# Six token tiles in one Sinkhorn chain on VectorE, instead of a second chain on GpSimd

## The chip, the cores and the metric

The kernel runs on one core of a Trainium2 chip. The metric is the device time of one execution in microseconds, the median of the runs. Besides the times there is one profiled execution, taken by the hardware profiler; all durations below come from it. Engines are named as in the profile: PE is TensorE, DVE is VectorE, ACT is ScalarE, POOL is GpSimd, SP is the engine that issues the DMAs.

## The reference, cut to what matters

Two adaLN layers follow each other on an input of 2 batch rows x 512 tokens x 512 features. Layer 0 is a gated linear attention with 32 heads and a feed-forward product. Layer 1 is an attention over the tokens, and then a mixing of four residual streams. That last step is where the change is made. For each token the 512 features are taken as n = 4 streams of C = 128:

```python
H_res_logits = (x_norm @ W_res.T).reshape(B, T, n, n) + H_res_base
H_pre  = softmax(x_norm @ W_pre.T  + H_pre_base)        # 4 per token
H_post = softmax(x_norm @ W_post.T + H_post_base)       # 4 per token
# Sinkhorn: 50 times rows, then columns, of a 4 x 4 matrix per token
u = -logsumexp(Z + v[..., None, :], axis=-1)
v = -logsumexp(Z + u[..., :, None], axis=-2)
H_res = (1 - g) * I + g * exp(Z + u[..., :, None] + v[..., None, :])
y = einsum('btnc,btn->btc', x_streams, H_pre) @ W_branch
out = einsum('btij,btjc->btic', H_res, x_streams) + einsum('btc,btn->btnc', y, H_post)
```

The 50 Sinkhorn steps of a token depend on each other; different tokens are independent. So the work is a long chain of very small instructions, each of which can take several token tiles at once.

## The kernel before

A token tile is 128 tokens, one on each partition. There are eight: tiles 0 to 3 of batch row 0 and tiles 0 to 3 of batch row 1. A framework schedules the traced instructions: priorities and a planned time line set a fixed order on each engine, and at run time each engine goes through its own list in that order, waiting on semaphores.

The last stage of the kernel begins when layer 1's attention has finished a half of a batch row (two tiles). For each pair of tiles there is then:

- `opening` (L966): transposes, a small product, statistics and the 24 logits of each token, the two softmaxes, and the branch `y` (tile `yb`).
- `first_iteration` (L1083): the first Sinkhorn step, with maxima and logarithms.
- `iterations` (L1106): the other 49 steps in linear form. A step is a product by the column factors (L1129), a sum of rows (L1119), a reciprocal (L1131), a product by the row factors (L1133), a sum of columns (L1119) and a reciprocal (L1135). Each needs the one before. After the steps named in `RENEW` (16 and 32) two logarithms and an exponential on ACT rebuild the matrix (L1139, L1111 to L1114).
- `result` (L1143): the mixing matrix (L1146, L1147, L1150).
- the mixing: `mixed_on_tensor` (L1171) writes 16 diagonal matrices per tile with ACT (L1161) and multiplies them on PE with the streams into one PSUM tile (L1182), and 4 more for the branch, unless the branch has been put into the PSUM tile before by `branch_on_tensor` (L1163). `mixed_on_vector` (L1197) does a tile with 16 DVE instructions (L1202) instead. `put` (L1153) multiplies by the gate on DVE (L1156), adds the residual on POOL or DVE (L1157) and stores the tile.

With `last=False` the products and sums of a chain run on POOL (L1129, L1133, L1122, L1123) and only the reciprocals run on DVE; with `last=True` everything runs on DVE.

Before the change the four pairs go like this:

- `streams0(0)` and `streams0(2)`: row 0, first and second half. Each has its own chain of two tiles on POOL (with reciprocals on DVE), and then its own two mixings on PE.
- `streams1a`: row 1, first half (called A below). It makes a room for four tiles, and runs steps 1 to 16 (`HEAD`) for its two tiles on DVE.
- `streams1b`: row 1, second half (called S below). After its `opening` and `first_iteration` it runs a joint chain of four tiles for 33 steps. Then A has had its 50 steps and is mixed, while S runs its last 16 steps with two tiles. At the end S's tile 1 is mixed on PE, its tile 0 on DVE.

`part(R, lo, hi)` takes some of the tiles of a room. `aside` (L1260) draws the next pieces of these generators into the trace, with raised priority.

Of the kernel before, what the change touches and what calls it, by code (L numbers as in the profile page):

```python
# [9 lines left out]
FP = mybir.dt.float32  # L10
# [6 lines left out]
UPS = 400, 400, 400, 400  # L17
RATES = None, None, None, None
HEAD = 16
UP = 400  # L20
# [16 lines left out]
P = 128  # L37
B, L, HID = 2, 512, 512
NC = L // P
# [4 lines left out]
NS, NITER = 4, 50  # L44
# [8 lines left out]
def tile_adaln(ctx: ExitStack, tc: tile.TileContext, a: dict, out: bass.AP):  # L53
    nc = tc.nc
# [6 lines left out]
    psp = ctx.enter_context(tc.tile_pool(name="ps", bufs=2, space=PSUM))  # L61
# [89 lines left out]
    def temp(shape, dt, name, bufs=2):  # L151
        return wk.tile(shape, dt, name=name, bufs=bufs)
# [202 lines left out]
    ps = bank([64, HID], "mps")  # L355
# [609 lines left out]

    def opening(S, last):  # L966

        b, c0, n = S["b"], S["c0"], S["n"]
        t0 = b * NC + c0
# [5 lines left out]
        for kc in range(KC):  # L975
            ps = psp.tile([P, n * P], FP, name="hps")
# [49 lines left out]
        nc.vector.tensor_tensor(sm, sm, m8.unsqueeze(3).to_broadcast(s8), ALU.mult)  # L1026
        yield

        yb = temp([P, 4, P], FP, "yb", 3)[:, 0:n]
        for c in range(n):  # L1030
            xp = temp([P, P], FP, "xp")
            if XP or b:
# [18 lines left out]
            yield  # L1051
        S.update(h=h, xs=xs, lg=lg, sm=sm, yb=yb)

# [6 lines left out]

    def chain_room(n, last):

        room = temp([P, 512], FP, "sinkhorn", 4)
        used = [0]

        def carve(shape):
            m = int(np.prod(shape[1:]))
            t = room[:, used[0]:used[0] + m]
            used[0] += m
            if len(shape) == 4:  # L1070
                return t.rearrange("p (c i j) -> p c i j", i=NS, j=shape[3])
            return t.rearrange("p (c i) -> p c i", i=NS)

        R = {k: carve([P, n, NS, NS]) for k in ("z", "t", "y", "K")}
        R.update({k: carve([P, n, NS]) for k in ("mx", "s", "u", "v", "fa", "fb", "fl")})
        if not last:
            R["pairs"] = carve([P, n, NS, 2])
        return R

    def part(R, lo, hi):  # L1080
        return {k: t[:, lo:hi] for k, t in R.items()}

    def first_iteration(S, R):  # L1083
        z, t, y, K, mx, s_, u, v, fl = (R[k] for k in ("z", "t", "y", "K", "mx", "s", "u", "v", "fl"))
        nc.vector.tensor_scalar(
            z, S["lg"][:, :, 0:16].rearrange("p c (i j) -> p c i j", j=NS), INV_TAU, None, ALU.mult
        )

        def minus_lse(dst, y, inv=None):
            nc.vector.tensor_reduce(mx, y, AX.X, ALU.max)  # L1090
            nc.vector.tensor_tensor(t, y, over(mx), ALU.subtract)
            act(t, t, AF.Exp)
            nc.vector.tensor_reduce(s_, t, AX.X, ALU.add)
            if inv is not None:
                nc.vector.reciprocal(inv, s_)
            act(s_, s_, AF.Ln)
            nc.vector.scalar_tensor_tensor(dst, mx, -1.0, s_, ALU.mult, ALU.subtract)

        minus_lse(u, z)
        yield  # L1100
        nc.vector.tensor_tensor(y, z, over(u), ALU.add)
        minus_lse(v, tp_(y), fl)
        nc.vector.tensor_tensor(K, tp_(t), along(fl), ALU.mult)
        yield

    def iterations(R, its, renew, last):  # L1106

        z, t, K, u, v, fa, fb, fl = (R[k] for k in ("z", "t", "K", "u", "v", "fa", "fb", "fl"))
        big = nc.vector if last else nc.gpsimd

        def kernel_of():  # L1111
            nc.vector.tensor_tensor(K, z, over(u), ALU.add)
            nc.vector.tensor_tensor(K, K, along(v), ALU.add)
            act(K, K, AF.Exp)  # L1114

        def sums(dst, y):

            if last:
                nc.vector.tensor_reduce(dst, y, AX.X, ALU.add)  # L1119
            else:  # L1120
                h2 = R["pairs"]
                nc.gpsimd.tensor_tensor(h2, y[:, :, :, 0:2], y[:, :, :, 2:4], ALU.add)  # L1122
                nc.gpsimd.tensor_tensor(dst, h2[:, :, :, 0], h2[:, :, :, 1], ALU.add)  # L1123

        for it in its:
            if it == 1 or it - 1 in renew:
                sums(fa, K)
            else:
                big.tensor_tensor(t, K, along(fb), ALU.mult)  # L1129
                sums(fa, t)  # L1130
            nc.vector.reciprocal(fa, fa)  # L1131
            yield
            big.tensor_tensor(t, tp_(K), along(fa), ALU.mult)  # L1133
            sums(fb, t)
            nc.vector.reciprocal(fb, fb)  # L1135
            if it in renew:
                for d, f in ((u, fa), (v, fb)):
                    act(fl, f, AF.Ln)
                    nc.vector.tensor_tensor(d, d, fl, ALU.add)  # L1139
                kernel_of()  # L1140
            yield

    def result(S, R):  # L1143

        hr, n = R["y"], S["n"]
        nc.vector.tensor_tensor(hr, R["K"], over(R["fa"]), ALU.mult)  # L1146
        nc.vector.tensor_tensor(hr, hr, along(R["fb"]), ALU.mult)  # L1147
        hrf = hr.rearrange("p c i j -> p c (i j)")
        for c in range(n):
            nc.vector.scalar_tensor_tensor(hrf[:, c, :], hrf[:, c, :], gt[:, 0:1], diag, ALU.mult, ALU.add)  # L1150
        S["hr"] = hr
# [10 lines left out]

    def branch_on_tensor(S, c):  # L1163

        S["ps", c] = mps = psp.tile([P, NS, P], FP, name="mixb", bufs=1)
        dg = wts.tile([P, NS + 1, P], FP, name="dg", bufs=2)
        for i in range(NS):
            diagonal(dg[:, i], S["sm"][:, c, 1, i:i + 1])
            nc.tensor.matmul(mps[:, i], lhsT=dg[:, i], rhs=S["yb"][:, c], start=i == 0, stop=False)
# [21 lines left out]
    def branch_on_scalar(S, c):  # L1191

        S["f", c] = f = wts.tile([P, NS, P], FP, name="foutb", bufs=1)
        for i in range(NS):
            nc.scalar.activation(f[:, i], S["yb"][:, c, :], AF.Copy, scale=S["sm"][:, c, 1, i:i + 1])
# [13 lines left out]

    RENEW = 16, 32  # L1210

    def streams0(c0):

        S = {"b": 0, "c0": c0, "n": 2}
        yield from opening(S, False)
        R = chain_room(2, False)
        yield from first_iteration(S, R)
        yield from iterations(R, range(1, NITER), RENEW, False)
        result(S, R)
        for c in range(2):  # L1220
            yield from mixed_on_tensor(S, c, nc.gpsimd)

    joint = {}

    def streams1a():

        S = joint["a"] = {"b": 1, "c0": 0, "n": 2}
        yield from opening(S, True)
        R = joint["R"] = chain_room(4, True)
        yield from first_iteration(S, part(R, 0, 2))  # L1230
        yield from iterations(part(R, 0, 2), range(1, HEAD + 1), (HEAD,), True)

    def streams1b(ahead):

        S = {"b": 1, "c0": 2, "n": 2}
        yield from opening(S, True)
        yield from ahead
        A, R = joint["a"], joint["R"]
        yield from first_iteration(S, part(R, 2, 4))
        branch_on_tensor(S, 1)  # L1240
        branch_on_scalar(S, 0)
        yield from iterations(R, range(1, NITER - HEAD), RENEW, True)
        result(A, part(R, 0, 2))
        side.append((None, mixed_on_tensor(A, 0, nc.gpsimd), UP))
        side.append((None, mixed_on_tensor(A, 1, nc.gpsimd), UP))
        yield from iterations(part(R, 2, 4), range(NITER - HEAD, NITER), RENEW, True)
        result(S, part(R, 2, 4))
        last = [mixed_on_tensor(S, 1, nc.vector), mixed_on_vector(S, 0)]
        while last:
            for e in list(last):  # L1250
                if next(e, "end") == "end":
                    last.remove(e)
            yield
# [4 lines left out]
    side = []  # L1258
# [51 lines left out]
    def weighed():  # L1310
        w = wt[0]
        wt[0] += 1
        if w < n_pieces:
            if w == n_pieces // 2:
                row_tiles(1, (GA,))
                values1(1)
            weigh(order[w // 8], w % 8)
        o = w - OUT
        if 0 <= o < n_pieces and o % 4 == 3:
            outputs(o // 4)  # L1320
        o -= 5
        if o >= 0 and o % 4 == 0 and o < n_pieces:
            j = o // 4
            finish(j)
            if j % 16 == 5:
                with behind():
                    row_tiles(j // 16, (SB, CB, GB))
                    weights24(j // 16)
            if j % 8 == 7:
                k = j // 8  # L1330
                if k == 2:
                    joint["ahead"] = streams1a()
                side.append((RATES[k], (streams0(2 * k) if k < 2 else joint["ahead"] if k == 2 else streams1b(joint["ahead"])), UPS[k]))

    virtual = []
    load_stationary("wk0", 0, 0)
# [37 lines left out]
    for n, u in enumerate(units):  # L1374
        g, b, c = u["at"]
# [128 lines left out]
```

## Time and profile before

| | |
|---|---|
| runs of the kernel before | 1398.12 us median of 3 (1397.33 to 1403.47) |
| the profiled execution | 1401.8 us; its span from first to last instruction is 1400.0 us |
| busy, share of the span | PE 89%, DVE 83%, ACT 59%, POOL 55% |
| granted TensorE clock, mean | 0.948 |

Busy time of the engines in five stretches of the end (from windows of the trace):

| stretch, us | what runs | PE | DVE | ACT | POOL |
|---|---|---|---|---|---|
| 1195 to 1258 | attention of row 1, both POOL chains | 59.40 | 55.37 | | 38.57 |
| 1258 to 1296 | end of attention, A's 16 steps, S's opening | 18.29 | 32.80 | 17.05 | 30.23 |
| 1296 to 1359 | the joint chain of four tiles | 11.44 | 54.95 | 14.98 | 44.70 |
| 1359 to 1387 | S's last 16 steps, mixings | 19.89 | 23.83 | 21.01 | 6.28 |
| 1387 to 1400 | the last tiles | 8.55 | 8.56 | 8.01 | 3.33 |

The shares over the whole span say little here: the change lies in the last 200 us, where other engines are busy than before. In a row of a timeline the first number is the start of the instruction, the second its duration, and the bracket at the end is the idle time of the engine before it with what ended it. An instruction's duration includes its latency, so two that don't depend on each other can overlap on one engine, and the step from one start to the next is what a chain pays. In a row of a group the numbers behind the bar are the busy time of the group and the mean ns of one.

### The profile page before, as it was taken

How to read it: one execution, taken by the hardware profiler on the slowest of the kernel's cores; microseconds unless marked ns; L12 is line 12 of the kernel's file. 1: busy time of each engine (PE TensorE's matmuls, PEld its weight loads, DVE VectorE, ACT ScalarE, POOL GpSimd, SP SyncE). 2: the span in 40 equal slices, each digit the busy share in tenths (PEclk: the TensorE clock that was granted, in tenths of full speed). 3: DMA queues.
4: the chain of work that ended last, by engine and by line, in shares of the span. 5: the costliest groups of instructions: out<-in, count | busy, mean ns of one | idle time of the engine just before them, and what ended most of it. 6: DMA issues, size and time to landing. Idle time of an engine off the chain costs nothing. (4 is left out here: it accounts for less than half of the span.)

```text
span 1400.0 us, 22901 instructions
## 1 busy us (share of the span) xinstructions
PE 1245.7 (89%) x7168; PEld 992.1 (71%) x7168; DVE 1159.8 (83%) x2969; ACT 831.5 (59%) x2354; POOL 775.8 (55%) x1169
## 2 busy tenths in 40 slices
PE   5979999999999999999988999799999889994128
PEld 3758888788788778888866777577676666663117
DVE  7998668687677687787899977688799979898887
ACT  5457576476376466666665656557567467664128
POOL 4454374364264367577777748545242655558861
PEclk9989999999999999999999999999999999997568
DMA  8022241231142343324333317523203231200001
GB/s 256 23 65 60 88 121 30 68 107 53 53 118 57 92 120 106 98 68 124 118 114 91 98 53 241 170 67 91 90 24 113 71 111 52 59 11 1 1 16 46
DMA packets 95377, 117.13 MB, mean 84 GB/s; under 512 B 10828, under 2 KB 50508, under 8 KB 95256
## 3 DMA queue, kind: packets, MB, share of 16 engines
q1 hardware_dynamic: 95256, 115.67, 27.7%
q8 instruction: 57, 0.93, 0.3%
q14 instruction: 64, 0.52, 0.1%
HBM read 102.11 MB, written 10.64 MB: 81 GB/s over the span
## 5 line engine op out<-in xcount | busy, mean ns | idle before, releaser
L846 DVE TENSOR_REDUCE m<-s 128x1 f32<-128x512 f32 x256 | 166.4, 673 | 18.6 <-PE s L842 18.3
L67 ACT ACTIVATE pt<-s 128x512 f32<-128x512 f32 x256 | 136.9, 602 | 33.3 <-PE s L876 31.7
L447 POOL TENSOR_TENSOR q<-xcos,rot 128x512 f32<-128x512 f32 x64 | 92.8, 1450 | 61.6 <-DVE xcos L445 57.1
L67 ACT ACTIVATE sg<-sg 128x512 f32<-128x512 f32 x128 | 80.6, 632 | 68.5 <-DVE sg L478 66.8
L876 PE MATMUL s<-qs,ks 100*128 100x256 f32 x512 | 103.3, 306 | 11.0 <-DMA qs<-mm 7.4
L842 PE MATMUL s<-ks,qs 96*128 96x512 f32 x256 | 103.6, 437 | 9.7 <-DVE m L846 7.5
L515 POOL TENSOR_TENSOR gb<-gb,q 128x512 f32<-128x512 f32 x48 | 63.2, 1319 | 77.7 <-ACT gb L67 68.7
L232 PE MATMUL pps<-hh,wq_h 128*128 128x512 f32 x256 | 103.2, 403 | 1.7 <-ACT vT L766 1.1
L876 PEld LDWEIGHTS s<-qs,ks 100*128 100x128 f32 x512 | 80.9, 195 | 33.5 <-ACT pt L67 8.9
L232 PE MATMUL gps<-wg_h,hh 128*128 128x512 f32 x256 | 101.8, 400 | 2.9 <-ACT wg_h L209 2.7
L232 PE MATMUL ops<-wo_h,zh 128*128 128x512 f32 x256 | 101.5, 397 | 1.7 <-ACT zh L570 1.0
L232 PE MATMUL ops<-wo_h,zl 128*128 128x512 f32 x256 | 100.8, 394 | 0.7 <-DVE zl L571 0.7
L232 PE MATMUL pps<-hl,wq_h 128*128 128x512 f32 x256 | 101.3, 396 | 0.0
L232 PE MATMUL pps<-hh,wq_l 128*128 128x512 f32 x256 | 101.2, 395 | 0.0
L232 PE MATMUL gps<-wg_l,hh 128*128 128x512 f32 x256 | 101.2, 395 | 0.0
L232 PE MATMUL gps<-wg_h,hl 128*128 128x512 f32 x256 | 100.6, 393 | 0.0
L232 PE MATMUL ops<-wo_l,zh 128*128 128x512 f32 x256 | 99.9, 390 | 0.0
L67 ACT ACTIVATE dec<-dec,room 128x128 f32<-128x128 f32 x256 | 83.0, 398 | 21.8 <-POOL dec L495 21.7
L548 PE MATMUL yps<-v,dec 128*128 128x128 f32 x512 | 94.2, 280 | 1.8 <-DVE xcos L445 1.0
L495 POOL TENSOR_SCALAR_AFFINE_SELECT dec<-gb 128x512 f32<-128x512 f32 x64 | 49.1, 768 | 80.7 <-DMA gb<-g_dram 51.8
L522 POOL TENSOR_TENSOR xw<-v,room 128x512 f32<-128x512 f32 x48 | 55.2, 1163 | 68.5 <-ACT v L462 64.3
L558 DVE SCALAR_TENSOR_TENSOR z<-yps,ss,sg 128x128 f32<-128x128 f32 x256 | 71.9, 340 | 24.0 <-ACT ss L67 23.8
(323 smaller groups left out, 3968.5 us busy)
## 6 DMA issues: line engine op xcount, KB each, us to landing
gb<-g_dram SPq DMA_DIRECT2D x64, 256.0 KB
raw<-in_wq SPq DMA_DIRECT2D x56, 256.0 KB
raw<-in_wg SPq DMA_DIRECT2D x48, 256.0 KB
raw<-in_wo SPq DMA_DIRECT2D x48, 256.0 KB
raw<-in_wmod SPq DMA_DIRECT2D x40, 256.0 KB
qs<-q_dram SPq DMA_DIRECT2D x64, 96.0 KB
q_dram<-hi SPq DMA_DIRECT2D x16, 256.0 KB
raw<-in_wk SPq DMA_DIRECT2D x14, 256.0 KB
```

The lines of the kernel that those rows point to most:

```text
L67: ins = nc.scalar.activation(o, i, func, **kw)
L232: nc.tensor.matmul(ps, lhsT=l, rhs=r, start=i == 0, stop=i == n - 1)
L447: nc.gpsimd.tensor_tensor(dst, sp(xc_), sp(rot), ALU.add)
L495: anchor["pool"] = nc.gpsimd.affine_select(out=dec, in_=gb, pattern=[[0, REP0], [1, P]], compare_op=ALU.is_ge, fill=-1e30, base=0, channel ...
L515: nc.gpsimd.tensor_tensor(gb, gb, q[:, c], ALU.mult)
L522: nc.gpsimd.tensor_tensor(xw, u["v"][:, c, :].unsqueeze(1).to_broadcast(sh4), wdc[:, c, r0:r0 + REP0].unsqueeze(2).to_broadcast(sh4), ALU. ...
L548: nc.tensor.matmul(yps[:, h, :], lhsT=u["pr"][:, h, :], rhs=u["v"][:, c, :], start=True, stop=not c)
L558: nc.vector.scalar_tensor_tensor(z[:, h, :], yps[:, h, :], ss[:, h:h + 1], sg[:, h * P:(h + 1) * P], ALU.mult, ALU.mult)
L842: anchor["pe"] = nc.tensor.matmul(ps, lhsT=st["qs"][rp][0:KS, i, qt * P:(qt + 1) * P], rhs=st["ks"][s][0:KS], start=True, stop=True,).ins
L846: anchor["dve"] = nc.vector.tensor_reduce(st["m"][:, 2 * qt + s, i:i + 1], ps, AX.X, ALU.max, negate=True).ins
L876: nc.tensor.matmul(ps[:, j, :], lhsT=st["ks"][s][0:KM, kt * P:(kt + 1) * P], rhs=st["qs"][rp][0:KM, i, :], start=True, stop=True,)
```

## The change

Row 0's second half no longer has a chain of its own on POOL. It does its `opening` and `first_iteration` at the same time as before, then waits, runs its steps 1 to 16 with A as a chain of four tiles on DVE, and the 33 joint steps with A and S as a chain of six tiles. After that four tiles (two of row 0, two of A) are mixed while S runs its last 16 steps. The branches of these four tiles and of S's tile 1 are put into five PSUM tiles during the joint chain. The room of a chain is sized by its number of tiles, and the branch tiles by two.

```diff
-        yb = temp([P, 4, P], FP, "yb", 3)[:, 0:n]
+        yb = temp([P, 2, P], FP, "yb", 4)
...
-        room = temp([P, 512], FP, "sinkhorn", 4)
+        room = temp([P, n * 128], FP, f"sinkhorn{n}", 1)
...
-        S["ps", c] = mps = psp.tile([P, NS, P], FP, name="mixb", bufs=1)
+        k = S["b"] * NC + S["c0"] + c
+        S["ps", c] = mps = psp.tile([P, NS, P], FP, name=f"mix{k}", bufs=1)
...
-    def streams0(c0):
-        S = {"b": 0, "c0": c0, "n": 2}
+    def streams0():
+        S = {"b": 0, "c0": 0, "n": 2}
...
-    def streams1a():
-        S = joint["a"] = {"b": 1, "c0": 0, "n": 2}
+    def streams1():
+        S = joint[1] = {"b": 0, "c0": 2, "n": 2}
+        yield from opening(S, False)
+        joint["R"] = chain_room(6, True)
+        yield from first_iteration(S, part(joint["R"], 0, 2))
+
+    def streams2():
+        S = joint[2] = {"b": 1, "c0": 0, "n": 2}
         yield from opening(S, True)
-        R = joint["R"] = chain_room(4, True)
-        yield from first_iteration(S, part(R, 0, 2))
-        yield from iterations(part(R, 0, 2), range(1, HEAD + 1), (HEAD,), True)
-
-    def streams1b(ahead):
+        R = joint["R"]
+        yield from first_iteration(S, part(R, 2, 4))
+        yield from iterations(part(R, 0, 4), range(1, HEAD + 1), (HEAD,), True)
+
+    def streams3(ahead):
         S = {"b": 1, "c0": 2, "n": 2}
         yield from opening(S, True)
         yield from ahead
-        A, R = joint["a"], joint["R"]
-        yield from first_iteration(S, part(R, 2, 4))
-        branch_on_tensor(S, 1)
-        branch_on_scalar(S, 0)
+        R = joint["R"]
+        yield from first_iteration(S, part(R, 4, 6))
+        before = [(joint[k], c) for k in (1, 2) for c in range(2)]
+
+        def branches():
+            for T, c in before + [(S, 1)]:
+                branch_on_tensor(T, c)
+                yield
+            branch_on_scalar(S, 0)
+            yield
+
+        def mixings():
+            for T, c in before:
+                yield from mixed_on_tensor(T, c, nc.gpsimd)
+
+        side.append((1, branches(), UP))
         yield from iterations(R, range(1, NITER - HEAD), RENEW, True)
-        result(A, part(R, 0, 2))
-        side.append((None, mixed_on_tensor(A, 0, nc.gpsimd), UP))
-        side.append((None, mixed_on_tensor(A, 1, nc.gpsimd), UP))
-        yield from iterations(part(R, 2, 4), range(NITER - HEAD, NITER), RENEW, True)
-        result(S, part(R, 2, 4))
+        for k in (1, 2):
+            result(joint[k], part(R, 2 * k - 2, 2 * k))
+        side.append((1, mixings(), UP))
+        yield from iterations(part(R, 4, 6), range(NITER - HEAD, NITER), RENEW, True)
+        result(S, part(R, 4, 6))
...
-                    joint["ahead"] = streams1a()
-                side.append((RATES[k], (streams0(2 * k) if k < 2 else joint["ahead"] if k == 2 else streams1b(joint["ahead"])), UPS[k]))
+                    joint["ahead"] = streams2()
+                work = (streams0, streams1, lambda: joint["ahead"], lambda: streams3(joint["ahead"]))[k]()
+                side.append((RATES[k], work, UPS[k]))
```

Below, R0a and R0b are row 0's first and second half.

## Prediction

> **What bounds the kernel now.** I read the page's slices first. The last five of forty (35 us each) have PE at 9, 4, 1, 2 and 8 tenths, while DVE stays at 8 or 9: after the attention the kernel is a DVE matter, with PE nearly idle.
>
> ```profile
> PE   5979999999999999999988999799999889994128
> ...
> DVE  7998668687677687787899977688799979898887
> ...
> POOL 4454374364264367577777748545242655558861
> ```
>
> Next the chain of waits, from its end backwards. It runs through ACT and PE from 1365.99 to the last two DVE rows, and before that through the small Sinkhorn rows.
>
> ```profile
> 1365.99 1.87 ACT dg L1161 x6
> 1367.90 10.37 PE mix L1182 x78
> 1378.27 0.93 PE mixb L1169 x8
> 1379.20 11.68 PE mix L1182 x80
> 1390.88 4.69 PE mixb L1182 x32
> 1395.59 0.70 DVE fout L1156
> ```
>
> What started it is in ACT's timeline:
>
> ```profile
> 1365.99 2.15 ACT L1161 ACTIVATE dg<-room,sinkhorn 128x128 f32<-128x128 f32 x7 [7.78 <-DVE sinkhorn L1150]
> ...
> 1390.24 4.77 ACT L1161 ACTIVATE dg<-room,sinkhorn 128x128 f32<-128x128 f32 x16
> ```
>
> ACT sat idle 7.78 us until R0b's result at 1365.7, although A's was there at 1360.3: R0b's diagonals stand first in its list. Then it wrote 100 diagonals (4 x 20, 4, 16) at 0.29 us each, 29 us, to 1395.0. So two chains share the end: DVE's long one to 1386.25, and R0b's on POOL, which then sets ACT. The joint chain runs from 1295.88 to 1359.35 (63.5 us) and A's head from 1259.55 to there.
>
> Last, DVE's timeline, for the price of a Sinkhorn step: the column product L1129 of four tiles, six steps apart, and of two tiles, four steps apart.
>
> ```profile
> 1344.97 0.23 DVE L1129 TENSOR_TENSOR sinkhorn<-sinkhorn 128x64 f32<-128x64 f32 x1
> ...
> 1355.32 0.26 DVE L1129 TENSOR_TENSOR sinkhorn<-sinkhorn 128x64 f32<-128x64 f32 x1
> ...
> 1366.71 0.19 DVE L1129 TENSOR_TENSOR sinkhorn<-sinkhorn 128x32 f32<-128x32 f32 x1
> ...
> 1372.25 0.19 DVE L1129 TENSOR_TENSOR sinkhorn<-sinkhorn 128x32 f32<-128x32 f32 x1
> ...
> 1374.68 1.26 DVE L1129 TENSOR_TENSOR sinkhorn<-sinkhorn 128x32 f32<-128x32 f32 x1
> ```
>
> (1355.32 - 1344.97)/6 = 1.725 us a step with four tiles, (1372.25 - 1366.71)/4 = 1.385 with two. Two more tiles cost 0.34 a step. The last row is a product that took 1.26 instead of 0.19: POOL's residual add (L1157, 1.28 us from 1374.62) ran beside it.
>
> **The sum, part by part**, against the profiled execution (1401.8 us; span 1400.0 and 1.8 around it).
>
> *Attention, to about 1258: 0.* Everything up to the middle of row 1's attention is in the same order. Then R0b's first 12 steps leave: 24 reciprocals on DVE (0.19 each) and some 17 us of POOL. PE is busy 59.40 of the 63 us from 1195 on, so PE, not those two, paces this stretch. At best its 3.6 idle us go; and since the scheduler places some score matmuls differently, I allow +3 the other way.
>
> *Head, 1259.55 to 1295.88 (36.3 us): +2.8.* The 16 steps now have four tiles. Alone, the chain was 16 x 1.385 = 22.2; the other 14.1 us are what 122 other DVE instructions between the last L846 and the joint chain add, 0.116 each. In the changed order 99 are left (24 reciprocals go, as does one renewal of two). So 16 x 1.725 + 99 x 0.116 = 39.1. Bounds: if the wider products only fill gaps, the removed instructions count alone (23 x 0.116 = -2.7); if those had been hidden, +5.4. S's `opening` ends at 1291.7, 4 us before the head, so it isn't what is late next.
>
> *Joint chain, 33 steps: +9.3.* No row shows six tiles. I continue the step from two to four: 1.725 + 0.34 = 2.06. The pieces are even: from start to start a product goes from 0.24 to 0.32, a sum from 0.22 to 0.25, a reciprocal from 0.24 to 0.29. 33 x 0.335 = +11.1; three steps have no L1129, -0.25. What else lay in the 63.5 us: 33 x 1.72 less three products is 55.8; the renewals took 3.5 and 1.4 us from the reciprocal (0.29 each of it counted already) to the next sum, the first because ACT's exponential stood behind R0a's diagonals and POOL was late; R0a's two `put`s cost 1.0 and 1.4; POOL's second chain 0.6 (14 steps at 1.765 instead of 1.72): together 63.1. After the change R0a's `put`s and the renewals stay; in ACT's new list 5 and 4 branch diagonals stand between the parts of the first renewal, at 0.29 each mostly beside DVE's own steps: 2.6 and 1.6, -0.7. The second POOL chain's 0.6 goes. I have 11.1 - 0.25 - 0.7 - 0.6 = +9.5, and take +9.3, since the result's first products fill gaps. The low bound of a step is the group means, which know nothing of waiting:
>
> ```profile
> L1119 DVE TENSOR_REDUCE sinkhorn<-sinkhorn 128x16 f32<-128x64 f32 x66 | 14.2, 214 | 1.8 <-ACT sinkhorn L67 0.3
> L1119 DVE TENSOR_REDUCE sinkhorn<-sinkhorn 128x8 f32<-128x32 f32 x64 | 11.3, 177 | 1.2
> ...
> L1133 DVE TENSOR_TENSOR sinkhorn<-sinkhorn 128x64 f32<-128x64 f32 x33 | 9.2, 280 | 0.7
> ...
> L1133 DVE TENSOR_TENSOR sinkhorn<-sinkhorn 128x32 f32<-128x32 f32 x32 | 7.0, 219 | 0.7
> ```
>
> A sum gains 37 ns, L1133 61, L1129 19 (240 to 259), the reciprocals 45: about 0.24 a step, +8.0 in 33 and 3.1 less than I take. The step in the timeline is nearer, for the chain waits at every instruction; a price over 0.34 I bound at 0.38 (+1.3).
>
> [...]
>
> *S's last 16 steps: +1.5.* Before, 26.9 us, of which 16 x 1.385 = 22.2 is the chain and 3.15 two `put`s (L1156 0.6 on DVE, and a product held up by L1157). Now four `put`s: one costs 1.0 to 1.6 without PE's wait, 1.35 x 4 = 5.4; four L1150 and two L1147 instead of two and one, +0.75 with the wider last reciprocal. 22.2 + 0.75 + 5.4 = 28.4. The mixings behind it: 64 diagonals x 0.29 = 18.8 us on ACT, covered by those 28. Were the cover gone (0.39 each, 25 us), it would still hold.
>
> *After S's last reciprocal: -3.1.* Before, 10.75 us (1386.25 to 1397.0), for ACT was behind. Now ACT is idle and starts S's 16 diagonals at once: 0.8 us to the result, then L1202's 16 (4.3) beside the diagonals (4.7), then two L1156 and two L1157 on DVE at 0.6 to 0.7: 7.65.
>
> *Early branch, `yb`, the room:* 20 diagonals (5.8 us of ACT) move from the end into the joint chain, where ACT is busy 14.98 of 63 us. Hidden; without that cover 5.8. The five PSUM tiles are taken when the attention's are free. R0b's pause after `first_iteration` holds no engine: its later steps are only placed later. Its two stores follow their `put`s on SP, where by then only stores stand, and the store behind the last `put` stays (1397.0 to 1400.0).
>
> Sum: 0 + 2.8 + 9.3 + 1.5 - 3.1 = +10.5, hence 1412.3 against 1401.8. The profiled run lies 0.26% above the median, so on 1398.12 I forecast 1398.1 + 10.5 = 1408.6.
>
> **The rivals.** (1) *Width is cheap*, which ends not slower: if a step of six tiles costs only 0.1 more than of four, 33 x 0.235 = 7.8 of the sum goes: 1400.8. It decides from a step under 1.95 us, where the sum falls below 7. For it: each instruction has a large part that does not grow (177 ns for a sum of 32). Against it: three kinds of instruction grew in the same ratio in the timeline. 0.13.
> (2) *Freed queues*: the attention gives its 3.6 and the head -2.7 instead of +2.8, 9.1 less: 1399.5. For it, POOL is at 30.23 of 38 us in the head and PE's L978 waits for its L931; against it, the head then was late, not the opening. 0.12.
> (3) *ACT's list*: the logarithm of joint step 16 stands behind R0a's 40 diagonals and 12 branch ones. R0a has 6 steps left when the joint chain starts, at 2.26 us each by the rows of POOL alone: 13.6 + 0.9 + 52 x 0.29 = 29.6, against 15.5 x 2.06 + 2.4 = 34.3. With a POOL step of 3.1 the slack of 4.7 is gone, and a later R0a costs what it is late: about +4, 1412.6. 0.13.
> That the change doesn't do what it says is out: in the built order DVE has 33 reciprocals L1131 of 24, and POOL has one chain.
>
> **The numbers.** My forecast has 0.62. A measurement of this kernel can tell about 0.5% (7 us) from no change. Slower by more: forecast and (3), 0.75. Within: most of (1) and (2), 0.20. Faster by 7 us would need both and a free head: 0.05. The range reaches from (1) and (2) to the upper bounds (+3 attention, +2.6 head): 1401 to 1414.5.
>
> **What would show it.** L1131 of 128x24 appears 33 times, L1129 of 128x96 starts 2.06 us apart; the joint chain begins at 1296 to 1300 and lasts about 73 us; ACT's last 16 diagonals follow an idle stretch; from S's last reciprocal to the end of DVE there are under 8.5 us. A step at 1.9 or less, or an attention that ends 3 us earlier, makes me wrong.

## The result, and the profile after

The changed kernel takes 1407.84 us (median of 20 runs, 1403.24 to 1412.01) against 1401.78 for the kernel before in the same comparison (1394.68 to 1407.02): a ratio of 1.0047 with the 95% interval 1.0032 to 1.0063. It is slower by a small amount, 6.06 us between the medians, which the interval sets apart from no change. Its profiled execution took 1408.9 us, with a span of 1407.1; the one of before 1401.8 and 1400.0.

Five marks on DVE cut the end of the two profiled executions in the same way: the first sum (L1119) of the head, of the joint chain, and of S alone, the end of S's last reciprocal, and the end of the last DVE instruction.

| stretch | before, us | after, us | difference | predicted |
|---|---|---|---|---|
| to the head's first sum | 1259.55 | 1257.28 | -2.3 | 0 |
| head, 16 steps | 36.33 | 36.89 | +0.6 | +2.8 |
| joint chain, 33 steps | 64.33 | 70.66 | +6.3 | +9.3 |
| S's last 16 steps | 26.24 | 28.62 | +2.4 | +1.5 |
| from S's last reciprocal to the end of DVE | 10.56 | 10.65 | +0.1 | -3.1 |
| sum | | | +7.1 | +10.5 |

(The prediction cut the joint chain from S's steps 0.9 us earlier; that much of its S stretch lies in the joint chain here.) The sum was too high by 3.4 us, and its terms were further off: head and joint chain were too high by 2.2 and 3.0, the end too low by 3.2, and the 2.3 us before the head had not been forecast.

The slices of the page of the changed kernel, as the prediction showed them of before, with the granted clock of PE:

```profile
PE   6979999999999999999988999899999899992515
...
DVE  7998678687677687787999977788799879889887
...
POOL 4353374364364367577687757544243644545201
PEclk9989999999999999999999999999999999995757
```

POOL is lighter in the last slices, as meant. PE ends 9, 2, 5, 1, 5: it works in two bursts with a pause before each, and in the last slices its clock is granted at 0.5 to 0.7.

DVE's timeline of the changed kernel, the column product of six tiles: eight steps while R0a's chain runs on POOL, and twelve when POOL is quiet.

```profile
1295.87 0.26 DVE L1129 TENSOR_TENSOR sinkhorn<-sinkhorn 128x96 f32<-128x96 f32 x1
...
1311.86 0.26 DVE L1129 TENSOR_TENSOR sinkhorn<-sinkhorn 128x96 f32<-128x96 f32 x1
...
1334.43 0.26 DVE L1129 TENSOR_TENSOR sinkhorn<-sinkhorn 128x96 f32<-128x96 f32 x1
...
1357.21 0.26 DVE L1129 TENSOR_TENSOR sinkhorn<-sinkhorn 128x96 f32<-128x96 f32 x1
```

(1311.86 - 1295.87)/8 = 2.00 us a step, (1357.21 - 1334.43)/12 = 1.898. The prediction had 2.06 for both. The groups of the chain, where the last number before the second bar is the mean ns of one:

```profile
L1119 DVE TENSOR_REDUCE sinkhorn<-sinkhorn 128x24 f32<-128x96 f32 x66 | 16.4, 249 | 3.0 <-ACT sinkhorn L67 1.2
L1133 DVE TENSOR_TENSOR sinkhorn<-sinkhorn 128x96 f32<-128x96 f32 x33 | 11.2, 338 | 1.0
L1131 DVE RECIPROCAL sinkhorn<-sinkhorn 128x24 f32<-128x24 f32 x33 | 9.9, 301 | 1.0
```

Against the four-tile rows the sum gained 35 ns (214 to 249), the product L1133 58 (280 to 338).

The chain of waits, from the last mixings on (start, duration, engine, tile, line):

```profile
1365.02 7.20 PE mix L1183 x32
1372.24 0.69 DVE fout L1156
1373.08 1.26 DVE sinkhorn L1129
...
1394.20 1.87 ACT dg L1161 x6
1396.11 6.55 PE mix L1183 x30
1402.69 0.70 DVE fout L1156
```

S's steps now set the end up to 1394, with four `put`s between them (a product beside POOL's add takes 1.26 instead of 0.19). Then, as predicted, ACT is idle and begins the last 16 diagonals at once. But PE's last 30 records (a product with a diagonal stands as two records in the trace, 32 for the 16 of a tile) take 6.55 us, and DVE waits for them:

```profile
1402.69 0.69 DVE L1156 TENSOR_TENSOR fout<-mix,row 128x512 f32<-128x512 f32 x1 [2.93 <-PE mix L1183]
```

In the windows of 2 us (time, length, busy us of PE, PE's weight loads, DVE, ACT, POOL, then the granted clock):

```profile
1386.00:1388.00 2.00, 0.00 (x0) 0.00 (x0) 1.86 (x7) 0.00 (x0) 0.46 (x1) 1.00 0.00 0
1388.00:1390.00 2.00, 0.00 (x0) 0.00 (x0) 1.82 (x6) 0.00 (x0) 0.80 (x1) 0.66 0.16 61
1390.00:1392.00 2.00, 0.00 (x0) 0.00 (x0) 1.70 (x9) 0.00 (x0) 0.00 (x0) 0.50 0.19 70
...
1398.00:1400.00 2.00, 2.00 (x11) 2.00 (x11) 1.69 (x4) 2.00 (x8) 0.00 (x0) 0.50 0.00 0
```

PE had nothing to do from 1385.68 to 1394.65. Some 3 us into that pause, at 1388.62, its clock went to 0.50, and it stayed there until 1402.28, for nearly all of the last tile.

So there are two theories. **POOL beside the chain**: the four-tile step of 1.725 from which I continued the slope contained a share that POOL's second chain cost, and width alone costs less. **The clock**: PE's pause, which the change makes, costs the end what ACT's earlier start gave. The rivals are that width gets cheaper as it grows, and that ACT's list or the buffers of the diagonals set the end.

### The profile page after: what moved, and what is told of

Its sections match the earlier page's. It is cut to its first block, busy times and chain, and to the rows that moved or that the text cites. A ratio compares the mean times of both kernels' runs of the same rounds, so it can differ in the third digit from the quotient of the medians.

```text
span 1407.1 us, 22530 instructions
## 1 busy us (share of the span) xinstructions
PE 1249.8 (89%) x7168; PEld 995.3 (71%) x7168; DVE 1164.7 (83%) x2863; ACT 830.5 (59%) x2348; POOL 717.3 (51%) x878
## 5 line engine op out<-in xcount | busy, mean ns | idle before, releaser
L1183 PE MATMUL mix<-h,dg 128*128 128x128 f32 x224 | 39.7, 345 | 66.9 <-ACT dg L1161 66.9
L554 ACT ACTIVATE z<-yps 128x128 f32<-128x128 f32 x256 | 67.4, 277 | 41.5 <-PE yps L550 28.2
```

Of the source, the lines that this page charges most:

```text
L554: nc.scalar.activation(z[:, h, :], yps[:, h, :], AF.Square, accum_out=ss[:, h:h + 1])
L1183: nc.tensor.matmul(mps[:, i], lhsT=dg[:, j], rhs=hv[:, j] if j < NS else yb[:, c], start=n > NS and j == 0, stop=j == n - 1 and (n > NS or ...
```

## Experiments: what a step costs

**The changed kernel without R0a's chain on POOL**, and **the kernel before without both**:

```diff
-        yield from iterations(R, range(1, NITER), RENEW, False)
+        yield from iterations(R, range(1, 3), RENEW, False)
```

> The changed kernel with R0a's chain on POOL cut to its first two linear steps (the other 47 Sinkhorn steps of that pair are left out), so that no POOL chain runs beside the joint chain. Theory 'POOL beside the chain' (part of a DVE step's time is what POOL's products and sums cost it): in the changed kernel the six-tile step takes 2.00 us while R0a's chain runs and 1.90 after it; here it takes 1.90 from its first steps on. Rival 'width alone' (the first steps are slow for another reason): they stay at 2.00.

> The kernel before with both POOL chains cut to their first two linear steps (47 Sinkhorn steps of row 0 are left out). Theory 'POOL beside the chain': the four-tile step, 1.725 us in the prediction's row, falls to about 1.64, the two-tile step stays at 1.385, and the slope from two to four tiles is then 0.26 us, the same as from four to six (1.90 - 1.64). Rival 'width alone': the four-tile step stays at 1.72, slope 0.34, and the six-tile step's 1.90 means that the slope flattens to 0.18.

DVE's timelines, the column product twelve steps apart in each, first of the changed kernel, then of the kernel before:

```profile
1303.85 0.26 DVE L1129 TENSOR_TENSOR sinkhorn<-sinkhorn 128x96 f32<-128x96 f32 x1
...
1326.58 0.26 DVE L1129 TENSOR_TENSOR sinkhorn<-sinkhorn 128x96 f32<-128x96 f32 x1
```

```profile
1302.73 0.23 DVE L1129 TENSOR_TENSOR sinkhorn<-sinkhorn 128x64 f32<-128x64 f32 x1
...
1322.38 0.22 DVE L1129 TENSOR_TENSOR sinkhorn<-sinkhorn 128x64 f32<-128x64 f32 x1
```

1.894 us with six tiles from the first steps on, 1.638 with four, and still 1.385 with two. That is 0.253 and 0.256 for two more tiles: a straight line. So 0.09 of the 1.725 was R0b's chain beside it. (The times of these kernels, 1410.0 and 1396.94 us in one run each, tell nothing: the cut pair is mixed during the attention, where PE is busy for 57.6 and 58.4 of the 60 us from 1200 on, and the joint chain starts 5 to 8 us later.)

The theory named POOL's products and sums as what costs the step. The trace points elsewhere: such a chain also has two reciprocals a step on DVE, and these stand in DVE's list between the instructions of the wide chain. In the changed kernel, from the reciprocal L1135 to the next column product, first with one of R0a's reciprocals (128x8) in between, then with none and with a POOL sum running when the product starts:

```profile
1299.42 0.30 DVE L1135 RECIPROCAL sinkhorn<-sinkhorn 128x24 f32<-128x24 f32 x1
1299.75 0.20 DVE L1131 RECIPROCAL sinkhorn<-sinkhorn 128x8 f32<-128x8 f32 x1
1299.87 0.21 DVE L1129 TENSOR_TENSOR sinkhorn<-sinkhorn 128x96 f32<-128x96 f32 x1
...
1301.38 0.30 DVE L1135 RECIPROCAL sinkhorn<-sinkhorn 128x24 f32<-128x24 f32 x1
1301.56 0.21 POOL L1122 TENSOR_TENSOR sinkhorn<-sinkhorn 128x16 f32<-128x16 f32 x1
1301.71 0.26 DVE L1129 TENSOR_TENSOR sinkhorn<-sinkhorn 128x96 f32<-128x96 f32 x1
```

The first takes 0.45 us from start to start, the second 0.33, as with POOL quiet (0.337). (R0a's reciprocal ends at 1299.95, 0.08 us after the start of the product behind it, which doesn't need it.) Over the prediction's row in the kernel before, the nine links of the chain with one of R0b's reciprocals in between took 0.36 us on the mean, the 27 others 0.26 (0.27 without POOL chains). No six-tile product of those eight steps that began while a POOL instruction of the chain ran took longer than with POOL quiet (six L1129 at 0.26, five L1133 at 0.32). The runs here take out POOL's work and the reciprocals together, so this division rests on the rows and not on a run.

**The kernel before without R0b's chain alone** (`range(1, NITER if c0 == 0 else 3)`, the room padded by 64 floats).

> The kernel before with R0b's POOL chain cut to two linear steps (47 steps of that pair are left out; the room is padded by 64 floats). It shows what the second POOL chain cost the attention and the head, where I forecast nothing: by the changed kernel's trace the head starts about 2 us earlier (1257.3 instead of 1259.6); A's 16 steps with two tiles should then take some 33 us instead of 36.3 if the second chain and its reciprocals were in the way, and 36 if S's opening beside it sets the pace. The four-tile step stays at 1.72 while R0a's chain runs and falls to 1.64 behind it if POOL is what costs, 1.72 throughout if width is.

The step took 1.77 on the mean of eight while R0a's chain ran, and 1.64 behind it, so one chain is enough. The other half of the question stayed open (one run, 1400.26 us): with R0b's mixing among the attention's matmuls the head began at 1259.4 and took 41.8 us, not 33, which says nothing of the chain that was taken out.

## Experiments: the end

**PE awake**, the changed kernel with something for PE in the pause (the operands shortened here):

```diff
+            if warm is not None and it >= NITER - 5 and it < NITER - 1:
+                pc = wts.tile([P, 2, NS], FP, name="pace", bufs=2)
+                act(pc, fa, AF.Copy)
+                nc.tensor.matmul(warm[0], lhsT=pc, rhs=warm[1], start=True, stop=True)
```

> The changed kernel, with one spare matmul of 512 columns after each of S's steps 45 to 48 (ACT copies that step's factors, so the matmuls are spread over the 9 us in which PE has nothing to do; their result is not used). Theory 'the clock': PE's granted clock is at 0.5 when S's 16 diagonals come, and their matmuls, not ACT, set the end; here the clock stays near 1, the last L1156 no longer waits 2.9 us for PE, the stretch from S's last reciprocal to the end of DVE falls from 10.85 to about 8 us, and the kernel gains about 3 us (ratio to the kernel before 1.0025 instead of 1.0047). Rival 'ACT's diagonals or their buffers set the end': 10.85 stays within 0.5.

**Four buffers** of diagonals (`name="dg", bufs=4`):

> The changed kernel with four instead of two buffers for the diagonals (and the chain's room padded by 32 floats). Theory 'the clock': ACT runs ahead, but PE at half clock still takes 6.5 to 7 us for the last 32 records, so the end stays at 10.85 within 0.7. Rival 'buffers': ACT's wait of 1.15 us in the last diagonals was the limit, and the end falls by 1.5 to 3 us.

PE awake brought 10.09 us for the end instead of 10.65, and a ratio of 1.0041 (1.0017 to 1.0064): a miss. The windows show why it is no answer yet:

```profile
1394.00:1396.00 2.00, 1.30 (x3) 0.10 (x2) 1.66 (x9) 0.21 (x1) 0.00 (x0) 1.00 0.00 0
1396.00:1398.00 2.00, 0.26 (x1) 0.26 (x2) 1.90 (x11) 0.72 (x3) 0.00 (x0) 0.84 0.00 0
1398.00:1400.00 2.00, 1.33 (x6) 1.04 (x6) 2.00 (x9) 1.73 (x6) 0.00 (x0) 0.50 0.00 0
```

The clock stayed at 1.00 through most of the pause and fell at 1397.36, just when the last tile's matmuls came: PE was only half busy before, and idle from 1395.73 to 1397.74.

Four buffers made the end longer, 12.18 us (one run, 1408.61 us), which neither theory had. PE's timeline shows the wait:

```profile
1392.79 0.80 PE L1183 MATMUL mix<-h,dg 128*128 128x128 f32 x2 [10.11 <-ACT dg L1161]
1396.58 5.74 PE L1183 MATMUL mix<-h,dg 128*128 128x128 f32 x30 [3.00 <-ACT dg L1161]
```

PE's second matmul waits 3 us for a diagonal, though ACT writes one each 0.29 us. At that pace PE's second diagonal is the 14th that ACT writes with four buffers, and the sixth in the changed kernel (hence "x6" in its chain). So ACT seems to write the first diagonal of the first group of four, then the groups for the other buffers, and only then the other three of the first. More buffers thus changed the order too, and this run does not test them alone; in the shorter head below ACT writes its last 16 diagonals with two buffers and no wait. The order of ACT's list is a small second cause in the changed kernel, by an estimate 4 x 0.29 = 1.2 us.

**PE full**: as PE awake, with 512 and 128 columns after each of steps 45 to 48, and 512 after the rows of the last step.

> The changed kernel with PE nearly full in the pause: after S's steps 45 to 48 a spare matmul of 512 and one of 128 columns, after the rows of step 49 one of 512 (in a_pe_awake PE was busy for 1.02 of each 1.5 to 2.5 us there, the granted clock stayed at 1.00 to 1397.3 and then still fell to 0.50 for the last 7.5 us). Theory 'the clock': it now stays at 1.00 to the end, the last 30 records take ACT's pace, about 4.4 us instead of 6.5, and from S's last reciprocal to the end of DVE there are 8 to 8.6 us instead of 10.65. Rival 'buffers and waits': over 9.8 us still.

PE's timeline, the last DVE wait, and a window of the end:

```profile
1391.73 1.02 PE L1136 MATMUL mix<-h,pace 128*8 128x512 f32 x2 [0.20 <-ACT pace L67]
1393.33 0.49 PE L1191 MATMUL mix<-h,dg 128*128 128x128 f32 x2 [0.57 <-ACT dg L1169]
1394.79 4.10 PE L1191 MATMUL mix<-h,dg 128*128 128x128 f32 x30 [0.97 <-ACT dg L1169]
```

```profile
1396.00:1398.00 2.00, 2.00 (x18) 2.00 (x18) 1.93 (x6) 2.00 (x8) 0.00 (x0) 1.00 0.00 0
```

```profile
1398.93 0.69 DVE L1164 TENSOR_TENSOR fout<-mix,row 128x512 f32<-128x512 f32 x1 [0.49 <-PE mix L1191]
```

The clock is at 1.00 up to the last matmul, the 30 records take 4.10 us instead of 6.54, the wait is 0.49 instead of 2.93, and the end takes 8.21 us instead of 10.65. The ratio falls to 1.0022 (1.0002 to 1.0041). The rows show the clock theory: the pause cost the end 2.4 us. (The intervals of this ratio and of 1.0047 overlap, so the times alone would not show it.)

## Experiments: the two halves of the change

**Six tiles without the early branch** of the four tiles (the branch list has only S's tile 1; the room padded by 64 floats):

```diff
-            for T, c in before + [(S, 1)]:
+            for T, c in [(S, 1)]:
```

> The changed kernel with six tiles in the chain, but the four earlier tiles' branches not put into PSUM early: 20 diagonals a tile again in the mixing behind the joint chain, as in the kernel before (S's tile 1 keeps its early branch; the room is padded by 64 floats). If early branches are hidden and useful: ACT's 80 diagonals take 23 to 24 us of S's last 30, so the end still waits for S's chain; PE is idle only some 4 us before S's diagonals. Theory 'the clock': with the shorter pause PE is partly awake and the end falls by up to 2 us, the first renewal gets shorter by 0 to 2 us: total -3 to 0 against the changed kernel, so a ratio of 1.0025 to 1.005 to the kernel before. Rival 'the early branches are what keeps the end short': later puts, +1 to +3 us.

**The early branch without six tiles**: the kernel before, its `branches` and `mixings` as in the change, for A's tiles and then R0b's.

> The kernel before with the other half of the change alone: two chains on POOL as before, but the branches of R0b's and A's four tiles are put into PSUM during the joint chain, and A's two tiles are mixed ahead of R0b's. ACT then has 32 + 32 + 16 diagonals from 1361 on instead of 100 from 1366: it is free by about 1380, so S's chain sets the end. Without the clock effect the end after S's last reciprocal would be 7.7 instead of 10.75, with it 10.5 to 11; four puts instead of two fall into S's last 16 steps, +2.7. Theory 'the clock': -1 to +3 us against the kernel before. Rival 'ACT's list was what bound the end': -3 us or better.

> As b_early_branch, with one spare matmul of 512 columns after each of S's steps 44 to 48 (paced by ACT copies of that step's factors; the result is not used). Theory 'the clock': 3 us better than b_early_branch, the last L1156 waits under 0.5 us for PE; against the kernel before -4 to 0. Rival: no difference to b_early_branch.

Without the early branch the joint chain takes 69.07 us instead of 70.66, S's steps 27.92 instead of 28.62, the end 10.15 instead of 10.65: 2.8 us less, and the ratio is 1.0023 (0.9999 to 1.0047). The first of these is in ACT's list at the first renewal, in the changed kernel:

```profile
1327.79 0.21 ACT L67 ACTIVATE sinkhorn<-sinkhorn 128x24 f32<-128x24 f32 x1
1327.90 1.55 ACT L1161 ACTIVATE dg<-room,sm 128x128 f32<-128x128 f32 x5
1329.36 0.21 ACT L67 ACTIVATE sinkhorn<-sinkhorn 128x24 f32<-128x24 f32 x1
1329.47 1.26 ACT L1161 ACTIVATE dg<-room,sm 128x128 f32<-128x128 f32 x4
1330.64 0.27 ACT L67 ACTIVATE sinkhorn<-sinkhorn 128x96 f32<-128x96 f32 x1
```

and without them:

```profile
1326.55 0.22 ACT L67 ACTIVATE sinkhorn<-sinkhorn 128x24 f32<-128x24 f32 x1 [2.49 <-DVE sinkhorn L1131]
1328.23 0.22 ACT L67 ACTIVATE sinkhorn<-sinkhorn 128x24 f32<-128x24 f32 x1 [1.46 <-DVE sinkhorn L1135]
1328.99 0.28 ACT L67 ACTIVATE sinkhorn<-sinkhorn 128x96 f32<-128x96 f32 x1 [0.54 <-DVE sinkhorn L1113]
```

Nine early diagonals stood between the two logarithms and the exponential, and DVE's chain waited for both:

```profile
1329.60 0.18 DVE L1139 TENSOR_TENSOR sinkhorn<-sinkhorn 128x24 f32<-128x24 f32 x1 [1.10 <-ACT sinkhorn L67]
1330.94 0.25 DVE L1119 TENSOR_REDUCE sinkhorn<-sinkhorn 128x24 f32<-128x96 f32 x1 [0.87 <-ACT sinkhorn L67]
```

The reciprocal L1135 of that step starts at 1327.84 in both profiles, and the exponential came 1.65 us later.

The early branch in the kernel before didn't help either: the joint chain stayed (64.65), S's steps got their two more `put`s (29.17, +2.9), and the end stayed long (10.08), with PE at a clock of 0.50 after a pause of 9.3 us. With half-busy spare matmuls the end was 10.06, as in the changed kernel: the same miss, so this run says nothing beyond that. In both the head also began some 5 to 7 us later than before (1264.8, 1266.9), and the ratios are 1.0051 (1.0028 to 1.0073) and 1.0057 (1.0033 to 1.0081), both worse than I had expected. What made the attention later I can't say; no run here separates that.

**Both remedies**, and then **the residual adds of the four tiles on DVE** (`mixed_on_tensor(T, c, nc.vector)`):

> a_no_early_branch with PE nearly full in its shorter pause (spare matmuls after steps 47, 48 and the rows of 49). If the two effects add, the end falls from 10.15 to about 8.2, and the kernel is 2 us better than a_no_early_branch: ratio 1.0005 to 1.002 to the kernel before. Rival: the end stays at 10 and the ratio at 1.002 to 1.003.

> As a_no_early_pe_full, with the residual add of the four mixed tiles on DVE (0.69 us each) instead of POOL. In the changed kernel a Sinkhorn product beside POOL's add (1.27) takes 1.03 to 1.26 instead of 0.19, so an add on POOL holds DVE for 0.84 to 1.07 us. If that is the whole of it, S's last 16 steps fall from 27.9 by 4 x 0.25 = 1.0 us: a ratio of about 1.000. Rival (POOL's add is free to the chain in part): +0.5 to +2 us.

Both remedies add: the end takes 7.86 us, and the ratio is 1.0002 (0.9982 to 1.0021). The change's loss is gone within that interval, and no gain is left. The adds on DVE are no gain: S's steps 28.97 instead of 28.58, ratio 1.0018 (1.0000 to 1.0035). Its end is longer too (9.48), since the clock fell at about 1397.8 in its profile, although it has the same spare matmuls: so they do not always hold the clock, and part of the worse ratio may be that.

**A shorter head.** One thing was left in the trace: S waits for the head.

```diff
-HEAD = 16
+HEAD = 13
...
-        side.append((1, branches(), UP))
-        yield from iterations(R, range(1, NITER - HEAD), RENEW, True)
+        yield from iterations(R, range(1, 20 + 1), (20, 34), True)
+        side.append((1, branches(), UP))
+        yield from iterations(R, range(20 + 1, NITER - HEAD), (20, 34), True)
...
+                with tc.high_priority(10 * (NS * NS - NS * i - j)):
```

> A version that puts the findings together. In the trace of the changed kernel S's first iteration is over at 1288.9, but the head of four tiles runs to 1294.2, so S waits 5 us: here HEAD is 13 instead of 16 (all tiles still get 50 steps), the joint chain has 36 steps, and S's last part 13. The early branches are put into PSUM only after the joint chain's first renewal, the renewals come after joint steps 20 and 34, so that no branch diagonal stands between them, PE is kept full before S's diagonals (spare matmuls after the last three steps), and a tile's diagonals keep their order on ACT. By the measured steps (1.64 with four tiles, 1.90 with six, 1.385 with two): three steps fewer in the head, -4.9, three more in the joint chain, +5.7, three fewer at the end, -4.2: -3.4 us; the renewal -1.6. Against a_pe_full (ratio 1.0022) -5 us, so a ratio of 0.9986 to the kernel before (0.997 to 1.0005). Rival: the head's steps only filled time in which S's opening held DVE, the joint chain starts less than 3 us earlier, and the ratio stays at 1.001 or more.

The ratio is 0.9963 (0.9940 to 0.9987): faster than the kernel before by a little, and better than the range that I had expected (0.997 to 1.0005), with a tile's diagonals in order on ACT by their priorities and the spare matmuls after the last three steps. The head takes 32.36 us, the joint chain 74.92, S's steps 23.28 and the end 7.63; against the changed kernel that is -4.5, +4.3, -5.3 and -3.0. ACT, PE and DVE at the end:

```profile
1388.97 4.79 ACT L1169 ACTIVATE dg<-room,sinkhorn 128x128 f32<-128x128 f32 x16 [1.20 <-DVE sinkhorn L1158]
```

```profile
1389.42 4.87 PE L1192 MATMUL mix<-h,dg 128*128 128x128 f32 x32 [0.58 <-ACT dg L1169]
```

```profile
1394.44 0.68 DVE L1164 TENSOR_TENSOR fout<-mix,row 128x512 f32<-128x512 f32 x1
```

PE follows ACT without a gap, and DVE's last product waits for nobody. Which of its five edits brings how much was not taken apart by runs, and the same edits were not tried on the kernel before.

## Why the prediction was right or wrong

**The time** (1408.6 forecast, 1407.84 measured) is right in large part by luck. The change was forecast at +10.5 us and is +6.06 between the medians; the absolute times agree because the kernel before, 1398.12 in the three runs that I started from, has a median of 1401.78 in twenty. Inside the sum, errors of both signs cancel as well. I gave 0.75 to slower by over 0.5% and 0.20 to less; the ratio, 1.0047 with its interval on both sides of that bound, lies just below it.

**Joint chain, +9.3 forecast, +6.3 measured.** The step that failed is "I continue the step from two to four". The two rows that I subtracted were not taken under the same conditions: beside the four-tile row R0b's chain ran, beside the two-tile row none did. In equal conditions two more tiles cost 0.255, so 33 x 0.255 = 8.4 instead of 11.1; the other 0.09 of the 0.34 was R0b's chain, by the rows its reciprocals on DVE. The low bound by group means, 0.24, was nearer than the value that I took. I did book 0.6 for POOL's second chain, from steps of 1.765 against 1.72, and so took for the quiet step one that was not quiet. The rest of the working together, -1.8 in the forecast, came to about -2.1 (6.3 - 8.4).

**Rival (1), width is cheap,** set its point at 1.95 us a step; the chain took 2.00 for the eight steps beside R0a's chain and 1.898 behind it, 1.92 on the mean, and my own test, "a step at 1.9 or less", went against me. It ended slower all the same, since the end did not give its 3.1.

**What grows with the width.** A large part of the 0.255 is the reciprocals: one takes 0.20 us for 8 elements, 0.25 for 16 and 0.301 for 24, so about 6.3 ns an element. Two of them in a step make 0.10 of the 0.255.

**Head, +2.8 forecast, +0.6 measured.** The same slope: with 1.64 for the step the formula gives 16 x 1.64 + 99 x 0.116 = 37.7, and 36.9 were measured. (The 1.725 had a POOL chain's reciprocals in it, and the 99 count such reciprocals again.)

**Attention, 0 forecast, -2.3 in the profile.** This can't be booked to the change: in the profiles of the changed kernel and of the seven others here that keep R0a's chain and put six tiles together, the head begins between 1255.6 and 1260.9, so a difference of 2 us between two profiles lies inside their spread. Rival (2), freed queues, is neither shown nor excluded.

**S's last 16 steps, +1.5 forecast, +2.4 measured:** `put`s, as forecast; the first waited 1.00 us for PE (0.48 in the kernel before), which began that burst at a clock of 0.50 (until 1371.56).

**The end, -3.1 forecast, +0.1 measured.** The step that failed is "L1202's 16 (4.3) beside the diagonals (4.7)": it lets PE follow ACT at 0.29 a diagonal. I asked what ACT would do when it was idle and not what the same pause does to PE. The rows were there: in the trace of before the clock is at 0.50 from 1362 to 1370, behind an idle stretch and into the work that follows (as above, the first number behind the length is PE's busy time, and 0.50 is the clock).

```profile
1362.00:1364.00 2.00, 0.00 (x0) 0.00 (x0) 1.61 (x10) 0.00 (x0) 1.25 (x6) 0.50 0.00 0
...
1368.00:1370.00 2.00, 2.00 (x9) 2.00 (x10) 1.69 (x10) 2.00 (x8) 0.00 (x0) 0.50 0.00 0
```

With PE kept full and the diagonals in order (the shorter head) the end took 7.83 us, counted like the working from the start of S's last reciprocal; the working had 7.65.

What the runs show of the clock is this. In the changed kernel it fell 2.9 us after the last matmul (1385.68 to 1388.62) and came back 6.2 us after the dense matmuls of the last tile began (1396.11 to 1402.28). By their windows of 2 us it fell some 2.1 us after the last matmul with the early branch in the kernel before, 3.9 without the early branch and 4.7 with four buffers, and came back some 5.0, 5.1 and 4.5 us after the dense matmuls began. In the profiles of the kernel before and of the changed one every spell of one clock (34 and 30, the first and the last, which the profile cuts, aside) lasts a whole multiple of 3.41 us, within 0.07. In the changed kernel PE was busy for 2.76 us of the 3.41 from 1395.45 to 1398.87, and the clock stayed at 0.50; it was busy for all of the next 3.41, and at their end, 1402.28, the clock was at 1.00 again. What makes it change no run shows.

**Early branch, "hidden".** On ACT's busy time it was. But I priced the first renewal with its nine diagonals at 2.6 us against 3.5 of before, and so booked a gain. It took 3.1 (1327.84 to 1330.94, from the reciprocal to the next sum), and 1.47 without them: the early branch by itself costs 1.6 there, and 1.2 in the stretches behind (0.7 in S's steps, for which no run shows why, and 0.5 at the end). **Rival (3)**, ACT's list, thus had the right place and too high a price.

## What to carry to other kernels

A price that is read from a chain's step holds for what ran beside it (here 1.725 us with R0b's chain, 1.638 with none): before two steps are subtracted, check in the timeline that the same work of other chains stood between their instructions in both. Work that is moved earlier leaves a pause behind; ask of PE whether it comes out of the pause at the clock that the next work is priced at (here at 0.50, where the last 30 records took 6.54 us instead of 4.10). And short work moved "under" a chain is only hidden if none of it stands in the same engine's list in front of something that the chain waits for (here nine diagonals cost the chain 1.6 us).

## What the runs showed of the hardware

- Two more tiles in a Sinkhorn step cost 0.253 and 0.256 us (1.385, 1.638 and 1.894 with two, four and six). A chain on POOL beside it makes each step 0.09 to 0.13 us longer (1.64 to 1.725 and 1.77), by the rows through its reciprocals on DVE: POOL's own short products and sums (0.20 to 0.27 us) did not lengthen a DVE product, while POOL's residual add (1.27) made a two-tile one of the changed kernel take 1.03 to 1.26 instead of 0.19 to 0.21.
- In PE awake, with PE busy for 1.02 us of each 1.5 to 2.5, the clock stayed at 1.00 for some 9 us more and then was 0.50 for about 7. With stretches of 1.24 us it held in three kernels and fell in one; where the limit lies no run shows.
- At 0.50 for nearly all of them the 30 records of the last tile take 6.54 us, at 1.00 4.10.
- In the profiles of the kernel before and of the changed one the clock was 0.50 or 1.00, in spells of whole multiples of 3.41 us (34 and 30 of them, the first and the last aside).
